# Moving a first pair of batches' outputs into the last two key-block pairs, and ordering products ahead of the moves out of their PSUM bank, in a one-core Perceiver block

## The chip, the core and the metric

The kernel runs on one core of one Trainium2 chip. A core has TensorE (PE: matrix products, with its weight loads shown apart as PEld), VectorE (DVE), ScalarE (ACT), GpSimd (POOL) and SyncE (SP, which here only issues transfers). Each engine works through its own instruction queue in order and waits on semaphores for the others. TensorE writes its results to PSUM, a memory of eight banks of 128 partitions by 512 float32 values; VectorE and ScalarE move them from there to SBUF, the main on-chip memory. DMA transfers between SBUF and HBM are issued from the queues of SP, ScalarE or GpSimd.

The metric is the device time of one execution in microseconds (us); lower is better.

## The reference, cut to what matters

All arithmetic is in float32. There are 4 batches of 256 tokens with 256 channels, and a context of 4096 rows with 192 channels for each batch. Three residual sublayers follow one another:

```python
x = x + cross_attention(layernorm(x), ctx)      # 16 heads of 16, 4096 keys
x = x + causal_self_attention(layernorm(x))     # 16 heads of 16, k and q normalised per head
x = x + slot_ffn(layernorm(x))                  # 64 slots, the 8 best for each token
```

The change is mostly in the third one:

```python
S = slot_init (64 slots, the same for each batch)
h = gelu(concat(x, mean(S)) @ w1 + b1)
logits = (h @ w2 + b2) / (abs(tau) + 0.1)
alpha = softmax over the 8 largest logits, 0 elsewhere        # tokens x slots
si = (alpha.T @ x) / alpha.sum(over tokens)                   # slots x channels
r, z = sigmoid(gates of si @ Wih.T + bih and S @ Whh.T + bhh)
n = tanh(i_n + r * h_n);  S_new = (1 - z) * n + z * S
y = layernorm(S_new + softmax(q(S_new) k(S_new).T / 8) v(S_new)) * ln_g + ln_b
out = alpha @ (y @ wvp + bvp) @ wo + bo
```

## The kernel before, in words

The order of the instructions on TensorE, VectorE and ScalarE is written out by hand: each queue holds its instructions in the order in which the Python code issues them, and a framework adds the waits. For PSUM it keeps engines apart by bank: a product into one half of a bank waits for a move out of the other half if the move was issued first.

Most of the time goes to the cross attention. Its 4096 keys come in chunks of 512, and the work is done in *blocks* of 128 keys and *pairs* of blocks: 16 pairs per batch, 64 in all. In a block (`cross_block`) TensorE computes scores into four pairs of banks (line 165), ScalarE takes their exponentials (line 1758 for the first pair of banks, in two halves; line 1760 for the three others), and TensorE weighs the values with them (line 179). The weighing of one pair is issued between the scores of the two blocks of the next pair. VectorE adds the weighed sums up (line 1774). The keys and values of the following chunk are computed meanwhile, in every pair but the last two, where no chunk follows.

The rest of the block is hung into these pairs by a dictionary, `plan`, with keys (batch of the loop, pair, place). While the loop goes through the keys of batch b, it does the remaining steps of batch b−1. From batch 1 on a loop has 17 pairs: pair 6 is the self attention of the previous batch (lines 1792, 1802 and 1823). Places 0 and 2 stand before the keys' or values' products of a pair, place 1 after them, place 4 at its end. A step gets the PSUM banks it may use; `x_` and `y` are the pairs of banks that the first and second exponentials of the pair's second block release. A step may be a generator; its later parts are issued at fixed points further on (`later`).

The steps that matter here, with their lines:

- Set-up, in the loop of batch 0: `set_logits` (line 1179) folds tau into `w2` and `b2` and the mean slot into `b1c`. `set_slots` (line 1203, three times) computes the gates' share that comes from the slots: two products into the two halves of one bank, and a move into `gh` after each (line 1212).
- Per batch: `self_out` makes `x2`, the input of the third sublayer; `hidden`, `routing` (line 1418 is its product) and `slot_inputs` (line 1460) follow, and `alpha_turned` (line 1486) makes `alphaT`, alpha transposed. Two batches share the partitions: an even batch has rows 0 to 63, an odd one rows 64 to 127.
- Per two batches: `gates` (three products with `wih`, each of half a bank, for r, z and n), `slot_qkv` with `slot_qk` and `slot_v` (q, k and v of the new slots), `slot_scores`, `slot_mix`, then `slot_values` (its result is `sv`, line 1630), and `give` for each batch: two products of `alphaT` with `sv` (line 1635), one addition of `x2` (line 1648), one transfer out (line 1640).

For batches 0 and 1, `gates` to `slot_mix` stand in the loop of batch 2 (pairs 13 to 16), `slot_values` in that of batch 3 at pair 5, and the two gives at its pairs 6 and 9. Batch 2's routing stands at pair 15 of batch 3, its `slot_inputs` and `alpha_turned` at pair 16.

After the last pair, `ending` (line 1864) does everything that is left: batch 3's last weighing (`cross_weigh`, into the two banks of `y`) and all its further steps, and the slots and outputs of batches 2 and 3 together. Each of its steps needs the one before. It ends with four products (lines 1635 and 2084), which give batch 3's and batch 2's outputs, two additions on VectorE (line 2095), two copies on ScalarE (line 2098) and four transfers, two from SP's queue and two from ScalarE's.

Where the listings number lines, these are the lines of the profile.

Of the kernel before, what the change touches and what calls it, by code (L numbers as in the profile page):

```python
# [900 lines left out]
def fast_(es, tc, nc, a, out, k, const, x0):  # L901
# [277 lines left out]
    def set_logits(bank):  # L1179
        rt = small.tile([P, 1], F32, name="rtau", tag="rtau")  # L1180
# [6 lines left out]

        m = small.tile([P, 2], F32, name="smean", tag="smean")
        nc.vector.tensor_reduce(m, slotsT[:, :, 0:SLOTS], AX.X, ALU.add)
        nc.vector.tensor_scalar(m, m, 1.0 / SLOTS, None, ALU.mult)  # L1190
        product(bank[:, 0:1], lambda c: w1[:, 2 + c, :], lambda c: m[:, c : c + 1])
# [11 lines left out]
    def set_slots(i, bank):  # L1203
        w = hold["whh"]
        for m in range(2):
# [4 lines left out]
            )  # L1210
            g = slice(2 * i + m, 2 * i + m + 1)
# [178 lines left out]
    def self_out(s, bank):  # L1390
# [6 lines left out]
        s.x2 = held.tile([P, QT, C], F32, name="x2", tag="x2")  # L1397
# [17 lines left out]
    def routing(s, bank):  # L1415

        for t in range(QT):
# [8 lines left out]
            small.tile([P, QT, n], F32, name=name, tag=name)  # L1426
# [66 lines left out]
    def gates(w, *room):  # L1493
# [5 lines left out]
        second = room[2] if len(room) > 2 else bank  # L1499
# [13 lines left out]
        pz = gate(2, second, int(second is bank))  # L1513
# [5 lines left out]
        pn = gate(4, other)  # L1519
# [15 lines left out]
    def slot_qk(w, bank, other):  # L1535
        w.fq, w.fk = (small.tile([DQ, S2], F32, name=n, tag=n, bufs=1) for n in ("fq", "fk"))
        q, k_ = bank[0:DQ, 0:S2], other[0:DQ, S2 : 2 * S2]
        for to, weights in ((q, fwq), (k_, fwk)):
            product(to, lambda c: weights[:, c, :], lambda c: w.snT[:, c, :])
        nc.scalar.activation(w.fq, q, AF.Identity, bias=fbq, scale=DQ**-0.5)  # L1540
        nc.vector.tensor_scalar(w.fk, k_, fbk, None, ALU.add)
# [7 lines left out]
    def slot_qkv(w, bank):  # L1549
        slot_qk(w, bank, bank)  # L1550
        slot_v(w, bank, 1)()
# [144 lines left out]
    for b in range(B - 1):  # L1696
# [5 lines left out]

        at = 4 if b == B - 2 else 0
# [17 lines left out]
            ((11 + at, 0), step(routing, s)),  # L1721
            ((12 + at, 0), step(slot_inputs, s)),
            ((12 + at, 1), step(alpha_turned, s)),
        ]
        if b % 2:
# [7 lines left out]
                ((NJ // 2 + 1 + 5, 0), step(slot_values, s.two)),  # L1733
                ((NJ // 2 + 1 + 6, 1), step(give, batches[b - 1])),
                ((NJ // 2 + 1 + 9, 1), step(give, s)),
            ]
        for (p, place), f in steps:
            plan[b + 1 + p // (NJ // 2 + 1), p % (NJ // 2 + 1), place] = f

# [124 lines left out]
    def ending(blocks, *pairs):  # L1864
# [134 lines left out]
        for t, bank in enumerate((x_0, x_1)):  # L1999
# [17 lines left out]
            held.tile([P, QT, C], F32, name=n, tag=n, bufs=b_) for n, b_ in (("x2", 2), ("x2n", 1))  # L2017
# [42 lines left out]
        slot_qk(both_, y_1, w_0)  # L2060
# [21 lines left out]
        for t, bank in enumerate((x_0, x_1)):  # L2082
            given(s, t, bank[:, 0:C])
            nc.tensor.matmul(
                w_1[:, t * C : (t + 1) * C],
                both_.alphaT[rows_of(d), t * P : (t + 1) * P],
                both_.sv[rows_of(d)],
                start=False,
                stop=True,
                skip_group_check=True,  # L2090
            )
        for t, bank in enumerate((x_0, x_1)):
            res, res_d = (temp()[:, 0:C].rearrange("p (t c) -> p t c", t=1) for _ in range(2))
            at = slice(t, t + 1)
            nc.vector.tensor_tensor(
                res, bank[:, 0:C].rearrange("p (t c) -> p t c", t=1), s.x2[:, at, :], ALU.add
            )
            nc.scalar.copy(res_d, halves(w_1)[:, at, :])
            send(s, at, res, nc.sync)
            send(d, at, res_d, nc.scalar)  # L2100
# [30 lines left out]
    for b, s in enumerate(batches):  # L2131
# [3 lines left out]
        for p in range(NJ // 2 + (b > 0)):  # L2135
# [22 lines left out]
            take(2, x_[:, 0, :], y[:, 1, :])  # L2158
            if not own and n + 1 < n_chunks:
# [74 lines left out]
```

## Time and profile before

| | |
|---|---|
| median of 3 runs | 860.78 us (857.23 to 861.16) |
| the profiled execution | 855.56 us |
| its span in the profile | 853.8 us |
| TensorE busy, share of the span | 826.6 us, 97% |
| ScalarE busy | 606.0 us, 71% |
| VectorE busy | 309.4 us, 36% |
| mean granted TensorE clock | 0.997 |
| written to HBM | 1.05 MB |

A line of a timeline gives the start in us from the span's start, the time until the last of its instructions ended, the engine, the line of the kernel and the operation, the tile written and the tiles read, the shapes, and how many instructions were merged into it (x16). A float32 product is recorded as two. In brackets stands how long the engine idled before it and what ended that wait. SPq and ACTq are the queues' own rows, here the issuing of transfers. All intermediate PSUM results are in one tile named `banks`.

### The profile page before, as it was taken

Reading aid. Unit: us, or ns where it says so; the run is one execution under the profiler, and the core shown is the slowest. Engines: PE = TensorE matmul, PEld = TensorE weight load, DVE = VectorE, ACT = ScalarE, POOL = GpSimd, SP = SyncE. Lnnn points to the kernel's source line nnn. Section 1 sums busy time; section 2 is a strip of 40 time slices with the busy share of each in tenths; the row PEclk is TensorE's granted clock in tenths of the full one; section 3 lists DMA queues with packets and bytes.
Section 4 is the critical chain, followed back from the end, with each engine's and each line's share of the span. In section 5 each row is a group of like instructions: output and inputs, shape, how many; then the busy total and the mean of one; then the engine's idle time right before and its main releaser. Section 6 shows DMA issues by size and latency. Waiting matters only on the chain.

```text
span 853.8 us, 18512 instructions
## 1 busy us (share of the span) xinstructions
PE 826.6 (97%) x7975; PEld 439.0 (51%) x7975; DVE 309.4 (36%) x760; ACT 606.0 (71%) x844; POOL 16.8 (2%) x20
## 2 busy tenths in 40 slices
PE   8999999999999999999999999989999999999885
PEld 5445545455555555545545555545555555444563
DVE  3133233232263352212254453232334433212664
ACT  5776766767677768777777777757777677877551
POOL 1000100000000010000000010000000000000000
PEclk9999999999999999999999999999999999999998
DMA  7600001000000000000000000000000101000000
GB/s 203 161 27 26 25 19 57 26 26 25 26 26 26 2 26 26 26 25 26 26 25 26 2 26 26 26 14 14 26 26 25 37 3 39 25 2 2 1 1 29
DMA packets 21850, 25.80 MB, mean 30 GB/s; under 512 B 6272, under 2 KB 13312, under 8 KB 21760
## 3 DMA queue, kind: packets, MB, share of 16 engines
q1 hardware_dynamic: 20800, 23.75, 9.6%
q8 instruction: 64, 1.05, 0.5%
q10 hardware_dynamic: 864, 0.79, 0.3%
q14 instruction: 26, 0.21, 0.1%
q0 software_dynamic: 96, 0.01, 0.0%
HBM read 23.48 MB, written 1.05 MB: 29 GB/s over the span
## 4 chain that ended last, share of the span: by engine, by line
PE 93%; ACT 3%; DVE 3%; issue 1%; ACTq 0%; DVEq 0%
PE banks L165 30%; PE banks L179 27%; PE banks L993 7%; PE banks L80 7%; PE banks L107 6%; PE banks L86 4%; PE banks L120 4%; PE banks L1823 1%; PE banks L981 1%; ACT prob L1760 1%; PE banks L194 1%; PE banks L1792 1%; PE banks L1460 1%; PE banks L1058 1%; ACT prob L1802 0%
## 5 line engine op out<-in xcount | busy, mean ns | idle before, releaser
L1760 ACT ACTIVATE prob<-banks 128x1024 f32<-128x1024 f32 x384 | 366.8, 1045 | 0.0
L165 PE MATMUL banks<-qh,kt 32*128 32x512 f32 x2048 | 267.3, 620 | 2.7 <-ACT prob L1760 1.5
L179 PE MATMUL banks<-prob,v 128*32 128x256 f32 x4096 | 234.3, 381 | 0.8 <-ACT prob L1802 0.5
L1758 ACT ACTIVATE prob<-banks 128x512 f32<-128x512 f32 x256 | 138.9, 595 | 131.4 <-PE banks L165 131.2
L179 PEld LDWEIGHTS banks<-prob,v 128*32 128x32 f32 x4096 | 126.6, 110 | 124.6 <-ACT prob L1758 45.8
L165 PEld LDWEIGHTS banks<-qh,kt 32*128 32x128 f32 x2048 | 103.9, 183 | 120.0 <-issue 69.2
L1774 DVE TENSOR_TENSOR sums<-banks,sums 128x512 f32<-128x512 f32 x120 | 82.6, 690 | 195.5 <-PE banks L179 166.4
L80 PE MATMUL banks<-ctx,wk 128*128 128x512 f32 x128 | 61.5, 603 | 0.1
L107 PE MATMUL banks<-wv,ctx 128*128 128x256 f32 x256 | 61.5, 383 | 0.0
L107 PEld LDWEIGHTS banks<-wv,ctx 128*128 128x128 f32 x256 | 46.9, 190 | 13.9 <-ACT prob L1758 6.8
L150 DVE COPY v<-banks 128x512 f32<-128x512 f32 x35 | 23.9, 690 | 79.9 <-PE banks L120 79.9
L94 DVE TENSOR_SCALAR kt<-banks,bk 128x512 f32<-128x512 f32 x32 | 24.0, 750 | 65.6 <-PE banks L86 65.6
L150 ACT COPY v<-banks 128x512 f32<-128x512 f32 x29 | 17.0, 586 | 32.7 <-PE banks L120 31.4
L86 PE MATMUL banks<-ctx,wk 64*128 64x512 f32 x128 | 37.0, 640 | 0.0
L95 ACT ACTIVATE kt<-banks,bk 128x512 f32<-128x512 f32 x32 | 22.1, 689 | 20.4 <-PE banks L86 19.6
L120 PE MATMUL banks<-wv,ctx 64*128 64x256 f32 x256 | 36.3, 402 | 0.0
L80 PEld LDWEIGHTS banks<-ctx,wk 128*128 128x128 f32 x128 | 20.9, 190 | 21.6 <-ACT prob L1760 11.9
L120 PEld LDWEIGHTS banks<-wv,ctx 64*128 64x128 f32 x256 | 22.0, 186 | 11.1 <-issue 9.6
L1807 DVE TENSOR_TENSOR prob<-prob,tri 128x512 f32<-128x512 f32 x32 | 20.8, 689 | 10.4 <-ACT prob L1802 9.8
L1802 ACT ACTIVATE prob<-banks 128x512 f32<-128x512 f32 (+1 forms) x30 | 17.9, 695 | 8.5 <-PE banks L1792 8.5
L987 DVE COPY tmp<-banks 128x512 f32<-128x512 f32 x17 | 11.8, 691 | 33.2 <-PE banks L981 33.2
L993 PE MATMUL banks<-wqkv,tmp 128*128 128x512 f32 (+1 forms) x64 | 23.0, 497 | 0.7 <-ACT prob L1802 0.5
(275 smaller groups left out, 505.6 us busy)
## 6 DMA issues: line engine op xcount, KB each, us to landing
ctx<-in_ctxT SPq DMA_DIRECT2D x32, 256.0 KB, 3.1
ctx<-in_ctxT SPq DMA_DIRECT2D x64, 128.0 KB, 3.2
x<-in_x SPq DMA_DIRECT2D x4, 256.0 KB, 3.4
wih<-in_ffn_WihT SPq DMA_DIRECT2D x1, 768.0 KB, 7.1
tmp<-in_ffn_WhhT SPq DMA_DIRECT2D x3, 256.0 KB, 5.7
out<-tmp SPq DMA_DIRECT2D x2, 256.0 KB, 2.2
wq<-in_L_xattn_Wq ACTq DMA_DIRECT2D x1, 256.0 KB, 5.9
wo<-in_L_xattn_Wo SPq DMA_DIRECT2D x1, 256.0 KB, 4.8
```

The lines of the kernel that those rows point to most:

```text
L80: nc.tensor.matmul(pk[c], k.wk[:, 0, c * P : (c + 1) * P], cx[:, 0, :], start=True, stop=False)
L86: nc.tensor.matmul(pk[c], k.wk[left(c), 1, c * P : (c + 1) * P], cx[left(c), 1, :], start=False, stop=True,)
L94: nc.vector.tensor_scalar(kt[:, 0, :], pk[0], k.bk[:, 0:1], None, ALU.add)
L107: nc.tensor.matmul(pv[n // 2][:, n % 2, :], cx[:, 0, n * P : (n + 1) * P], k.wv[:, 0, :], start=(n % 2 == 0), stop=False, skip_group_check ...
L120: nc.tensor.matmul(pv[u][:, i, :], cx[left(u), 1, n * P : (n + 1) * P], k.wv[left(u), 1, :], start=False, stop=True, skip_group_check=True,)
L150: copy(v[:, :, 0 : H * VW].rearrange("p i (h w) -> p i h w", w=VW)[:, :, :, 0:D], src.rearrange("p i (h d) -> p i h d", d=D),)
L165: nc.tensor.matmul(sc[:, m, :], kt[r, c, i * P : (i + 1) * P], qh[r, c, :], start=True, stop=True)
L179: nc.tensor.matmul(po[q * 32 : (q + 1) * 32, s * NQ : (s + 1) * NQ], v[:, i, w0 : w0 + 32], pr[s][:, m, e * NQ : (e + 1) * NQ], start=(fir ...
L993: nc.tensor.matmul(dst, lhs(c), rhs(c), start=(c == 0), stop=(c == 1))
L1758: nc.scalar.activation(pt[:, m, :], sc[:, m, :], AF.Exp)
L1760: nc.scalar.activation(pt, sc, AF.Exp)
L1774: nc.vector.tensor_tensor(s.sums[c], bank, s.sums[c], ALU.add)
```

## The change

It has these parts:

1. `set_logits`: the mean slot and its product are issued ahead of the six steps with tau.
2. `set_slots`: both products are issued before the two moves.
3. `gates`, where it has two banks: the second product goes to the other bank, and the third to the second half of the first bank.
4. `slot_qkv`: the products of q, k and v are issued first, then the three moves; for batches 0 and 1 the move of q (`fq`) goes from ScalarE to VectorE.
5. `slot_values` of batches 0 and 1 goes to pair 15 of batch 3's loop, ahead of batch 2's routing; their two gives go to pair 16, behind batch 2's `alpha_turned`. A new place 5 gives them four banks, after the second block's scores; the two gives use the banks that the last weighing uses next. Batch 2's routing, `slot_inputs` and `alpha_turned` move from places 0 and 1 to place 5 of the same pairs.
6. `x2` has three buffers in place of two; the four large tiles of `routing` have one in place of two.
7. `ending`: the four last products alternate between batches 2 and 3, with one bank for each batch; one addition, one copy and two transfers of 256 KB follow, batch 2's from SP's queue and batch 3's from ScalarE's.

```diff
     def set_logits(bank):
+        m = small.tile([P, 2], F32, name="smean", tag="smean")
+        nc.vector.tensor_reduce(m, slotsT[:, :, 0:SLOTS], AX.X, ALU.add)
+        nc.vector.tensor_scalar(m, m, 1.0 / SLOTS, None, ALU.mult)
+        product(bank[:, 0:1], lambda c: w1[:, 2 + c, :], lambda c: m[:, c : c + 1])
         rt = small.tile([P, 1], F32, name="rtau", tag="rtau")
...
-        m = small.tile([P, 2], F32, name="smean", tag="smean")
-        nc.vector.tensor_reduce(m, slotsT[:, :, 0:SLOTS], AX.X, ALU.add)
-        nc.vector.tensor_scalar(m, m, 1.0 / SLOTS, None, ALU.mult)
-        product(bank[:, 0:1], lambda c: w1[:, 2 + c, :], lambda c: m[:, c : c + 1])
         nc.vector.tensor_tensor(b1c, bank[:, 0:1], b1, ALU.add)
...
                 lambda c: slotsT[:, c, :],
             )
+        for m in range(2):
             g = slice(2 * i + m, 2 * i + m + 1)
             nc.vector.tensor_scalar(
                 gh[:, i, m, :],
...
-        s.x2 = held.tile([P, QT, C], F32, name="x2", tag="x2")
+        s.x2 = held.tile([P, QT, C], F32, name="x2", tag="x2", bufs=3)
...
-            small.tile([P, QT, n], F32, name=name, tag=name)
+            small.tile([P, QT, n], F32, name=name, tag=name, bufs=1)
             for name, n in (("lg", SLOTS), ("rest", SLOTS), ("best", 8), ("ex", SLOTS))
...
         bank, other = room[0], room[1]
-        second = room[2] if len(room) > 2 else bank
+        second = room[2] if len(room) > 2 else other
...
-        pz = gate(2, second, int(second is bank))
+        pz = gate(2, second)
...
-        pn = gate(4, other)
+        pn = gate(4, other if len(room) > 2 else bank, int(len(room) == 2))
...
-        nc.scalar.activation(w.fq, q, AF.Identity, bias=fbq, scale=DQ**-0.5)
-        nc.vector.tensor_scalar(w.fk, k_, fbk, None, ALU.add)
+
+        def move():
+            if w.last:
+                nc.scalar.activation(w.fq, q, AF.Identity, bias=fbq, scale=DQ**-0.5)
+            else:
+                nc.vector.tensor_scalar(w.fq, q, DQ**-0.5, fbq, ALU.mult, ALU.add)
+            nc.vector.tensor_scalar(w.fk, k_, fbk, None, ALU.add)
+
+        return move
...
     def slot_qkv(w, bank):
-        slot_qk(w, bank, bank)
-        slot_v(w, bank, 1)()
+        moves = slot_qk(w, bank, bank), slot_v(w, bank, 1)
+        for move in moves:
+            move()
...
-            ((11 + at, 0), step(routing, s)),
-            ((12 + at, 0), step(slot_inputs, s)),
-            ((12 + at, 1), step(alpha_turned, s)),
         ]
+        if b < B - 2:
+            steps += [
+                ((11, 0), step(routing, s)),
+                ((12, 0), step(slot_inputs, s)),
+                ((12, 1), step(alpha_turned, s)),
+            ]
...
-                ((NJ // 2 + 1 + 5, 0), step(slot_values, s.two)),
-                ((NJ // 2 + 1 + 6, 1), step(give, batches[b - 1])),
-                ((NJ // 2 + 1 + 9, 1), step(give, s)),
...
+    def first_more(x_0, x_1, y_0, y_1):
+        slot_values(batches[0].two, x_1)
+        return routing(batches[B - 2], x_0)
+
+    def second_more(x_0, x_1, y_0, y_1):
+        s = batches[B - 2]
+        slot_inputs(s, x_0)
+        alpha_turned(s, x_1)
+        for e, bank in zip(batches, (y_0, y_1)):
+            give(e, bank)
+
+    plan[B - 1, 15, 5], plan[B - 1, 16, 5] = first_more, second_more
...
-        for t, bank in enumerate((x_0, x_1)):
-            given(s, t, bank[:, 0:C])
-            nc.tensor.matmul(
-                w_1[:, t * C : (t + 1) * C],
...
-        for t, bank in enumerate((x_0, x_1)):
-            res, res_d = (temp()[:, 0:C].rearrange("p (t c) -> p t c", t=1) for _ in range(2))
-            at = slice(t, t + 1)
-            nc.vector.tensor_tensor(
-                res, bank[:, 0:C].rearrange("p (t c) -> p t c", t=1), s.x2[:, at, :], ALU.add
-            )
-            nc.scalar.copy(res_d, halves(w_1)[:, at, :])
-            send(s, at, res, nc.sync)
-            send(d, at, res_d, nc.scalar)
+        for t in range(QT):
+            for e, bank in ((d, w_1), (s, x_0)):
+                r = rows_of(e)
+                nc.tensor.matmul(
+                    bank[:, t * C : (t + 1) * C],
+                    both_.alphaT[r, t * P : (t + 1) * P],
+                    both_.sv[r],
+                    start=(e is s),
...
+        res, res_d = (halves(temp()) for _ in range(2))
+        nc.scalar.copy(res_d, halves(w_1))
+        nc.vector.tensor_tensor(res, halves(x_0), s.x2, ALU.add)
+        send(d, slice(0, QT), res_d, nc.sync)
+        send(s, slice(0, QT), res, nc.scalar)
...
             take(2, x_[:, 0, :], y[:, 1, :])
+            take(5, x_[:, 0, :], x_[:, 1, :], y[:, 0, :], y[:, 1, :])
```

## The prediction

> **What bounds the kernel now.** I read the page first, for the engine that fills the span and the chain that ended last; then the waits of each tile that the edit touches; then the timelines around those waits; then the last 80 us engine by engine.
>
> ```profile
> PE 826.6 (97%) x7975; PEld 439.0 (51%) x7975; DVE 309.4 (36%) x760; ACT 606.0 (71%) x844; POOL 16.8 (2%) x20
> ...
> PE 93%; ACT 3%; DVE 3%; issue 1%; ACTq 0%; DVEq 0%
> ```
>
> TensorE works through one fixed queue, and 93% of the chain is that queue. ScalarE, at 71%, waits for it in every pair of key blocks. So until the last two pairs, time taken out of TensorE's queue comes off the end. In the last two pairs and in the ending, dependencies decide. The timeline near 565 us shows the largest stall:
>
> ```profile
> 564.30 2.08 PE L165 MATMUL banks<-qh,kt 32*128 32x512 f32 x16
> 566.43 2.86 ACT L1760 ACTIVATE prob<-banks 128x1024 f32<-128x1024 f32 x3
> 566.79 0.60 PE L993 MATMUL banks<-snT,fwk 128*64 128x128 f32 x4
> 569.14 0.37 ACT L1540 ACTIVATE fq<-banks,fbq 64x128 f32<-64x128 f32 x1
> 569.54 0.34 DVE L1541 TENSOR_SCALAR fk<-banks,fbk 64x128 f32<-64x128 f32 x1 [3.55 <-ACT fq L1540]
> 569.94 1.13 PE L993 MATMUL banks<-fwv,snT 128*128 128x256 f32 x4 [2.54 <-DVE fk L1541]
> ```
>
> ScalarE's move of fq stands behind three exps; fk shares its bank and waits for it; TensorE's next product is in that bank too and waits for both. Smaller stalls of the same kind, a product waiting for the move out of its own bank, stand at the slot products and at the gates:
>
> ```profile
> 120.19 0.71 PE L993 MATMUL banks<-slotsT,tmp 128*128 128x128 f32 x4
> 121.47 0.71 PE L993 MATMUL banks<-slotsT,tmp 128*128 128x128 f32 x4 [0.56 <-DVE gh L1212]
> ...
> 552.24 1.16 PE L993 MATMUL banks<-siT,wih 128*128 128x128 f32 x8
> 553.98 2.05 PE L993 MATMUL banks<-siT,wih 128*128 128x128 f32 x16 [0.59 <-DVE gate_r L1511]
> ```
>
> The last two pairs have no keys and values to compute:
>
> ```profile
> 777.62 0.66 PE L1418 MATMUL banks<-w,hT 128*128 128x64 f32 x4
> 779.76 2.90 PE L165 MATMUL banks<-qh,kt 32*128 32x512 f32 x16 [1.48 <-ACT prob L1760]
> ...
> 788.31 2.86 ACT L1760 ACTIVATE prob<-banks 128x1024 f32<-128x1024 f32 x3
> 789.73 0.65 PE L1486 MATMUL banks<-ident,alpha 128*64 128x128 f32 x4
> 790.31 3.66 PE L179 MATMUL banks<-prob,v 128*32 128x256 f32 x64
> 790.75 0.29 DVE L1472 TENSOR_TENSOR siT<-banks,sden 128x128 f32<-128x128 f32 x1
> ```
>
> At 778 TensorE idles 1.48 us for an exp to release a bank; at 790 it goes from batch 2's transposed alpha into the last weighing with no gap.
>
> **The change, part by part.** I count by when TensorE's next instruction starts, since a recorded length holds a drain that overlaps its successor.
>
> *Slot set-up (three times).* A product that nothing delays hands over 0.54 us after its start (1.08 for the eight rows at 552.24). The second products now start then: 121.47 − 120.73 = 0.74, and by the same rows at 132.47 and 145.18 0.75 and 0.68. Sum −2.17. VectorE's first move starts 0.3 us later and the second earlier; what follows uses other banks.
>
> *Mean ahead of tau.* The product starts at 109.23; TensorE was done with the scores of 106.75 at about 108.75. The six tau and scale steps (107.56 to 108.64) go behind. Reduce (0.28) and scale (0.17) then end near 108.2: −0.48. w2, b2 and b1c are first used a batch later.
>
> *Gates.* The second gate goes to the other bank, which the third exp of the block releases at about 553.4. TensorE is ready at 553.30, so 0.15 us remain of 0.68: −0.53. The third gate takes the first bank's second half; gate_r's addition (553.50 to 553.92) is over before the second gate's product (about 554.5).
>
> *q, k and v before their moves.* TensorE could go on at 567.27 (k's product hands over after 0.48, as q's does from 566.31 to 566.79) and goes on at 569.94: −2.67. fq leaves ScalarE for VectorE, where it costs what fk does (0.34). The moves now wait for the product of v (568.3): fq, fk and fv end near 569.5. Behind them waits the scores product, which TensorE reaches at 572.73 − 2.67 = 570.06, so the cover is 1 us for fk; each microsecond beyond comes back. VectorE was idle there for 3.55 us.
>
> *Outputs moved out of batch 3's pairs 5, 6 and 9.* slot_values goes (666.46 to 667.42: −0.96), the first give (679.44 to 680.50: −1.06), and the second, which ran among key products: those take 1.92 us there (713.54 to 715.46) against 1.06 two pairs earlier (689.98 to 691.04), −0.86. Sum −2.88. ScalarE idles 0.9 to 2.4 us before the next groups of exps there, so it does not take the gain. Two additions leave VectorE and two sends SP's queue; the context loads there wait for TensorE anyway.
>
> *slot_values before the routing, pair 15.* 0.96 us. It waits for the second half of the first exp (777.9) and ends near 778.9, the routing near 779.6; the scores behind it wait for the exp until 779.76. I take 0; with the cover gone it is +0.96. VectorE's sv (0.48) and logits end near 780, and ScalarE takes the routing's exp only at 784.60.
>
> *The gives, pair 16.* TensorE now runs four products at 790.31 (their bank is free at 789.4), and the last weighing, in those same banks, waits for VectorE's addition of each. The first give takes 1.13 (row at 679.44), to 791.44; VectorE is through with siT at 791.04; the addition takes 0.69 (L1648's median, 688 ns), to 792.17. The weighing starts at 792.2 instead of 790.31: +1.9. The second addition ends near 792.9 and is needed at 794.0. Below: at the ending VectorE's addition starts 0.79 us after the first such product (844.33 to 845.12); 0.79 + 0.69 = +1.5. Above: the gives start only with the last exp's end at 791.17: +2.8. Everything behind is the ending, so this is all on the path. ScalarE's alphaT copy now waits for the gives (one buffer, old rows read first): from 791.02 to about 792.4; behind it stands a 1.28 us table load, and ScalarE's next work is at 795.95. SP's two sends wait for VectorE with nothing urgent behind them.
>
> *Buffers.* A third x2 holds batch 0's rows longer. The routing tiles go to one buffer; their uses are a batch apart, or 38 us before the last (788.1 against 826.6). 0.
>
> *The last transfers.*
>
> ```profile
> 845.58 1.92 SPq L1640 DMA_DIRECT2D out<-tmp  x2
> 846.43 0.37 ACT L2098 COPY tmp<-banks 128x256 f32<-128x256 f32 x1 [0.46 <-ACT tmp L2098]
> 846.83 0.66 ACTq L1640 DMA_DIRECT2D out<-tmp  x1
> ```
>
> Before, the last of four issues is at 846.83 and lands in 2.6 us. After, one copy (0.59 as for other 512-wide copies) and one addition (0.69) start at 845.5, so both issues come by 846.25. A 256 KB store landed in 2.2 us alone; with two at once I allow 3.1, as for the 128 KB ones on SP: 848.5 to 849.4 against 849.4. I take −0.2; bounds −0.9 and +0.5. The Trainium skill, "DMA: Bandwidth & Descriptors", section "Issuing engines are not separate DMA queues", says that queues share the same 16 DMA engines, so a second issuing engine saves only issue time. By that rule the same bytes leaving 0.5 us later end 0.5 us later, and the sum below would be −6.3; the rows of 846 to 849 us (143, 125, 273 GB/s) leave it open.
>
> **Sum:** −2.17 − 0.48 − 0.53 − 2.67 − 2.88 + 0 + 1.9 − 0.2 = −7.0 us. The profiled execution took 855.56 (span 853.8), so its like would take 848.6. It lies 5.2 below the median of the runs, 860.78, so against that median I say 853.8.
>
> **Rivals.**
> *The last pairs cost more:* +2.8 and +0.96 in place of +1.9 and 0. For it: both waits hang on ScalarE's release of banks. Against: the releases are 0.9 us early at both places. Gain 5.1, 855.7.
> *Part comes back:* stalls are counted in full only if the banks behind them are free; if a third of the 8.7 us taken out returns as waits for exps, and the last pairs cost 2.8, the gain is 5.8 − 2.8 + 0.2 = 3.2: 857.6, within 0.5% (4.3 us, about what a measurement tells from no change).
> *The exps pace the pairs:* then nothing taken out of TensorE's queue before pair 15 counts, and the added +1.9 remains: 862.5, slower than before; with the upper costs 2.8, 0.96 and 0.5, 865.0. It decides where ScalarE idles less per pair than TensorE loses. Against it: ScalarE idles 1.7 to 2.1 us before most second blocks, and after 569.5 for 3.86 us, more than each stall.
> *The transfers end later* (+0.5): 854.5.
>
> **Chances.** The forecast with its bounds, the dearer last pairs and the later transfers give gains over 4.3: 0.78. Part comes back: 0.16. Paced by exps: 0.06, of which I put all on slower to be safe. The range: with all bounds good the gain is 8.7 − 1.5 + 0.9 = 8.1, which from the lowest run, 857.23, gives 849.1; the profiled execution's like, 848.6, lies a little lower, so the low end is 848.5. With a third of the 8.7 back, dear last pairs and late transfers it is 5.8 − 2.8 − 0.5 = 2.5, from the median 858.3; the high end is 858.5.
>
> **What would show it.** After: no wait of TensorE on gh or fk; the gate wait near 0.15; no slot_values before pair 15 of batch 3; the gap at 778 filled; the last weighing released by VectorE's tmp about 0.8 us after the last give; two stores at the end. The prediction is wrong if the score products after the removed stalls wait longer for ScalarE than now, or if the last weighing starts over 3 us after the alpha product.

## The result, and the profile after

The kernel after takes 849.32 us (median of 4 runs, 848.42 to 850.32), where the kernel before took 859.28 beside it (4 runs, 857.23 to 861.16). The ratio is 0.9889, with a 95% interval from 0.9858 to 0.9919: 10.0 us faster. The prediction was 853.8 us and a gain of 7.0: right in sign and inside its range, but 4.5 us too high in time. The profiled execution of after took 850.10 us, with a span of 848.2; that of before had 853.8. So the two profiles differ by 5.6 us only, and the timed runs by 10. Both gaps, 5.6 against the predicted 7.0 and 10.0 against 7.0, have to be explained.

The page of after, its busy times and its chain of work:

```profile
PE 828.2 (98%) x7975; PEld 440.2 (52%) x7975; DVE 309.1 (36%) x760; ACT 605.7 (71%) x842; POOL 16.7 (2%) x20
...
PE 94%; ACT 2%; DVE 2%; issue 0%; ACTq 0%; DVEq 0%
```

TensorE bounds the kernel as before; its share of the chain rose from 93% to 94%, at the cost of the waits for ScalarE and VectorE (3% each before). It is even 1.6 us longer busy than before, although nothing was added to its work; the reason is below.

The timeline of after around the slots, the gates and q, k and v (start, time until the last ended, engine, line, operation; in brackets the idle time before and what ended it):

```profile
120.81 1.16 PE L993 MATMUL banks<-slotsT,tmp 128*128 128x128 f32 x8
...
550.39 3.26 PE L993 MATMUL banks<-siT,wih 128*128 128x128 f32 x24
...
563.93 0.65 PE L993 MATMUL banks<-snT,fwq 128*64 128x128 f32 x4
...
564.42 0.60 PE L993 MATMUL banks<-snT,fwk 128*64 128x128 f32 x4
564.95 1.13 PE L993 MATMUL banks<-fwv,snT 128*128 128x256 f32 x4
565.91 1.89 PE L107 MATMUL banks<-wv,ctx 128*128 128x256 f32 x8
566.19 0.34 DVE L1546 TENSOR_SCALAR fq<-banks,fbq 64x128 f32<-64x128 f32 x1 [2.58 <-PE banks L993]
566.46 0.33 DVE L1547 TENSOR_SCALAR fk<-banks,fbk 64x128 f32<-64x128 f32 x1
566.72 0.40 DVE L1555 TENSOR_TENSOR fv<-banks,fbv 128x256 f32<-128x256 f32 x1
567.73 0.33 PE L1567 MATMUL banks<-fk,fq 64*64 64x64 f32 x4
```

The eight slot products and the 24 gate products are each one unbroken group; no product waits for gh, gate_r or fk. TensorE goes from q to k to v and on to the values without a pause. VectorE's three moves run beside it, and the score product at 567.73 waits for none of them.

The timeline of after in the last two pairs:

```profile
770.64 1.13 PE L993 MATMUL banks<-w,yT 128*128 128x256 f32 x4 [0.24 <-ACT prob L1780]
771.61 0.55 PE L1419 MATMUL banks<-w,hT 128*128 128x64 f32 x4
772.48 2.90 PE L165 MATMUL banks<-qh,kt 32*128 32x512 f32 x16 [0.31 <-ACT prob L1782]
...
782.44 0.65 PE L1487 MATMUL banks<-ident,alpha 128*64 128x128 f32 x4
783.02 1.14 PE L1644 MATMUL banks<-sv,alphaT 64*128 64x256 f32 x8
784.24 0.36 ACT L1492 COPY alphaT<-banks 64x256 f32<-64x256 f32 x1 [0.35 <-PE banks L1644]
784.25 1.29 DVE L1657 TENSOR_TENSOR tmp<-banks,x 128x512 f32<-128x512 f32 x2 [0.50 <-PE banks L1644]
785.00 3.66 PE L179 MATMUL banks<-prob,v 128*32 128x256 f32 x64 [0.84 <-DVE tmp L1657]
```

The gap of 1.48 us ahead of the scores of pair 15 is now 0.24 + 0.31, with slot_values in it. The four products of the gives start at 783.02, and the last weighing waits 0.84 us for VectorE's first addition: it starts 1.98 us after the gives began, where before it had no gap.

The last products before, and the timeline of the end after:

```profile
844.33 0.48 PE L1635 MATMUL banks<-sv,alphaT 64*128 64x256 f32 x1
```

```profile
840.09 1.13 PE L2107 MATMUL banks<-sv,alphaT 64*128 64x256 f32 x8
841.31 0.58 ACT L2116 COPY tmp<-banks 128x512 f32<-128x512 f32 x1 [2.12 <-PE banks L2107]
841.37 0.69 DVE L2117 TENSOR_TENSOR tmp<-banks,x 128x512 f32<-128x512 f32 x1 [1.38 <-PE banks L2107]
841.92 0.37 SPq L1649 DMA_DIRECT2D out<-tmp  x1
842.09 0.40 ACTq L1649 DMA_DIRECT2D out<-tmp  x1
```

The two issues stand 1.83 and 2.00 us behind the start of the last products; before, the last of four stood 2.50 us behind it (844.33 to 846.83).

This profile also has something that the first profile of before lacks. Busy time by stretch in the ending of after (columns: stretch, its length, busy time of PE, PEld, DVE, ACT and POOL with counts, granted clock of TensorE, DMA share, GB/s):

```profile
823.00:824.00 1.00, 0.03 (x1) 0.03 (x1) 0.81 (x4) 0.00 (x0) 0.00 (x0) 1.00 0.00 0
824.00:826.30 2.30, 2.30 (x18) 2.06 (x19) 1.07 (x3) 0.16 (x1) 0.00 (x0) 1.00 0.00 0
826.30:829.70 3.40, 3.40 (x18) 3.40 (x18) 1.31 (x4) 0.62 (x2) 0.00 (x0) 0.51 0.00 0
```

For 3.4 us TensorE runs at half its clock, in the gates' 24 products, which take 4.57 us instead of 2.94. (That is also why it is longer busy.) The first profile of before has no such stretch ahead of its last product.

**A measure for all profiles.** To compare profiles I use four times of each: S, the start of the first transposes (L981; it moves by up to 1.5 us between executions), W, the start of the last weighing, F, the start of the last products, and the end of the span. W − S holds all pairs, F − W the ending, the tail what follows. "Half clock" says where TensorE ran at half clock for one such stretch, ahead of F.

| kernel | S | W − S | F − W | tail | half clock |
|---|---|---|---|---|---|
| before (first profile) | 6.75 | 783.56 | 54.02 | 9.47 | none |
| before_again | 6.73 | 783.55 | 54.03 | 9.69 | none |
| before_third | 7.03 | 784.95 | 54.01 | 9.81 | pair 15 |
| before_fourth | 7.33 | 785.09 | 54.04 | 9.94 | pair 15 |
| setup_only | 7.09 | 781.53 | 54.03 | 9.85 | pair 15 |
| qkv_only | 6.62 | 781.21 | 54.04 | 9.83 | none |
| moves_only | 7.09 | 783.16 | 55.35 | 9.80 | ending |
| end_only | 6.87 | 784.86 | 54.04 | 8.53 | pair 15 |
| before_gap_filled | 7.57 | 783.58 | 55.40 | 9.65 | ending |
| after (first profile) | 7.83 | 777.17 | 55.09 | 8.11 | ending |
| after_again | 8.00 | 777.20 | 55.31 | 8.09 | ending |
| after_warm | 6.98 | 777.19 | 53.96 | 8.17 | none |
| gives_late | 6.77 | 775.22 | 56.13 | 7.98 | ending |
| gives_late_pe | 6.55 | 775.38 | 53.96 | 8.01 | none |

The pairs lost 783.56 − 777.17 = 6.39 us, and the tail 9.73 (mean of the four profiles of before) − 8.1 = 1.6. That makes 8.0. Against it, the first profile of after started 1.08 us later (S) and lost 1.07 in the ending to the half clock: 8.0 − 2.2 = 5.8, and the 5.6 between the spans, with the tail of before's first profile at 9.47, is explained.

### The profile page after: what moved, and what is told of

Read it like the earlier page. It is cut to its first block, busy times and chain, and to the rows that moved or that the text cites. A ratio compares the mean times of both kernels' runs of the same rounds, so it can differ in the third digit from the quotient of the medians.

```text
span 848.2 us, 18509 instructions
## 1 busy us (share of the span) xinstructions
PE 828.2 (98%) x7975; PEld 440.2 (52%) x7975; DVE 309.1 (36%) x760; ACT 605.7 (71%) x842; POOL 16.7 (2%) x20
## 4 chain that ended last, share of the span: by engine, by line
PE 94%; ACT 2%; DVE 2%; issue 0%; ACTq 0%; DVEq 0%
PE banks L165 30%; PE banks L179 27%; PE banks L993 7%; PE banks L80 7%; PE banks L107 7%; PE banks L86 4%; PE banks L120 4%; PE banks L1845 1%; PE banks L981 1%; PE banks L194 1%; PE banks L1058 1%; ACT prob L1782 1%; PE banks L1814 1%; PE banks L1461 1%; ACT prob L1824 0%
```

## The experiments

The theories were these. *Rows*: the gain is the sum of the parts as the timelines show them. *Clock*: a part of what the timed runs differ by is stretches at half clock, which come and go behind gaps of TensorE. *Part comes back* and *the last pairs cost more* are rivals of the prediction.

**setup_only**: parts 1 to 3 of the change on the kernel before.

```diff
+        product(bank[:, 0:1], lambda c: w1[:, 2 + c, :], lambda c: m[:, c : c + 1])
         rt = small.tile([P, 1], F32, name="rtau", tag="rtau")
...
+        for m in range(2):
             g = slice(2 * i + m, 2 * i + m + 1)
...
-        second = room[2] if len(room) > 2 else bank
+        second = room[2] if len(room) > 2 else other
```

> Parts 1 to 3 alone (mean slot ahead of tau, slots' products ahead of their moves, gates' banks in turn). The theory 'rows' (time leaves TensorE's queue as the timelines of the two kernels show it: mean 0.46, slots 2.45, gates 0.54): 3.45 us faster than before, 0.996 of it; the prediction's own terms give 3.18. The theory 'part comes back' (a third returns as waits for exps): 2.3 us. The theory 'clock' (some of what the whole change gained is stretches at half clock that come or go with the phase of the work): the runs of one kernel fall into groups with granted clocks 0.001 to 0.003 apart, 1 to 2 us each, and the median can lie 1 to 2 us off the rows' figure to either side.

Median 854.9 us against 858.6, ratio 0.9955 (0.9933 to 0.9978). Its profile has a stretch at half clock in pair 15, as before_third and before_fourth have; against these two W − S falls from 785.02 to 781.53, that is 3.49. Rows said 3.45, the prediction's terms 3.18: nothing came back.

**qkv_only**: part 4 alone.

```diff
-        slot_qk(w, bank, bank)
-        slot_v(w, bank, 1)()
+        moves = slot_qk(w, bank, bank), slot_v(w, bank, 1)
+        for move in moves:
+            move()
```

> Part 4 alone (products of q, k, v ahead of their moves, fq on VectorE). 'Rows': 2.62 us faster (the prediction said 2.67), 0.997. 'Part comes back': 1.8 us. 'Clock', if the stall of 2.54 us at 567 us is what lowers the clock in the timed runs of before: up to 2 us more, 4.5 us, and a granted clock in this kernel's runs above that in the runs of before. The timeline at 565 us should show no wait of TensorE between the products of q, k and v.

Median 853.61 us, ratio 0.9937 (0.9917 to 0.9958): 5.0 us faster, twice what the rows give. In the profile the pairs around the edit move from +0.11 to −2.50 us against before, which is 2.61, as rows said; W − S fell by 2.35. The rest of the median goes with the clock: none of its six runs lay under 0.996, and against the three runs of before beside it that reached 0.997 (mean 855.6) its mean, 853.6, is 2.1 lower. With six runs I can't say that this edit keeps the clock up; it may be chance.

**moves_only**: parts 5 and 6 alone.

```diff
-                ((NJ // 2 + 1 + 5, 0), step(slot_values, s.two)),
-                ((NJ // 2 + 1 + 6, 1), step(give, batches[b - 1])),
-                ((NJ // 2 + 1 + 9, 1), step(give, s)),
...
+    plan[B - 1, 15, 5], plan[B - 1, 16, 5] = first_more, second_more
```

> Parts 5 and 6 alone (outputs of the first two batches in pairs 15 and 16, three buffers for x2). 'Rows', from the two kernels' timelines: pairs 5, 6 and 9 give 0.90 + 0.68 + 0.86 = 2.44, pair 16 takes 1.97: 0.5 us faster. The prediction's terms: 2.88 - 1.9 = 1.0 faster. 'The last pairs cost more': 0.9 slower. 'Clock': any of these plus or minus 1 to 2 us.

Median 857.69 us, ratio 0.9984 (0.9964 to 1.0005): the runs alone show no change. W − S falls by 0.40: rows, within 0.1. By itself this part is worth next to nothing in work: it takes 2.4 us out of the pairs and puts 1.98 us on the path to the last weighing. But all twelve runs lay between 856.47 and 859.43 us, at clocks of 0.994 to 0.996, while 10 of 24 runs of before beside it lay between 860.8 and 863.9, at 0.988 to 0.991. Busy time by stretch in the ending of moves_only:

```profile
835.30:836.80 1.50, 0.23 (x2) 0.00 (x0) 1.33 (x4) 0.10 (x1) 0.00 (x0) 1.00 0.00 0
836.80:838.50 1.70, 1.09 (x8) 0.86 (x9) 0.39 (x2) 0.36 (x1) 0.00 (x0) 1.00 0.00 0
838.50:841.90 3.40, 3.38 (x13) 2.68 (x13) 1.75 (x7) 1.69 (x3) 0.00 (x0) 0.50 0.00 0
```

The pause of 1.37 us that TensorE makes ahead of q's product (836.90) and one of 0.53 us ahead of the slots' scores (838.52) stand right before the half clock.

**end_only**: part 7 alone.

```diff
-            send(s, at, res, nc.sync)
-            send(d, at, res_d, nc.scalar)
+        res, res_d = (halves(temp()) for _ in range(2))
...
+        send(d, slice(0, QT), res_d, nc.sync)
+        send(s, slice(0, QT), res, nc.scalar)
```

> Part 7 alone (two transfers of 256 KB at the end, one copy, one addition). The prediction: 0.2 us faster (between 0.9 faster and 0.5 slower; by the rule that the bytes leave 0.5 us later, 0.5 slower). 'Rows', from the two profiles (last product to end of span 9.5 us before, 8.1 after): 1.36 us faster, 0.998. If neither, the profile's last issue and the stretch behind it show which of the two moved.

Median 856.7 us, ratio 0.9978 (0.9954 to 1.0001): by the runs alone the gain is not clear of noise. The tail is 8.53 us, against 9.47 to 9.94 in four profiles of before: 1.2 less, near the rows' 1.36 and far from the prediction's 0.2. The last issue starts 0.50 us earlier. Busy time by stretch behind the products, before:

```profile
846.50:847.00 0.50, 0.00 (x0) 0.00 (x0) 0.00 (x0) 0.30 (x1) 0.00 (x0) 1.00 0.75 256
847.00:847.50 0.50, 0.00 (x0) 0.00 (x0) 0.00 (x0) 0.00 (x0) 0.00 (x0) 1.00 0.68 227
847.50:848.00 0.50, 0.00 (x0) 0.00 (x0) 0.00 (x0) 0.00 (x0) 0.00 (x0) 1.00 0.08 23
848.00:848.50 0.50, 0.00 (x0) 0.00 (x0) 0.00 (x0) 0.00 (x0) 0.00 (x0) 0.55 0.94 334
848.50:849.00 0.50, 0.00 (x0) 0.00 (x0) 0.00 (x0) 0.00 (x0) 0.00 (x0) 0.50 0.64 211
```

and end_only:

```profile
848.50:849.00 0.50, 0.00 (x0) 0.00 (x0) 0.00 (x0) 0.00 (x0) 0.00 (x0) 1.00 0.89 311
849.00:849.50 0.50, 0.00 (x0) 0.00 (x0) 0.00 (x0) 0.00 (x0) 0.00 (x0) 1.00 0.98 336
849.50:850.00 0.50, 0.00 (x0) 0.00 (x0) 0.00 (x0) 0.00 (x0) 0.00 (x0) 1.00 1.00 342
850.00:850.50 0.50, 0.00 (x0) 0.00 (x0) 0.00 (x0) 0.00 (x0) 0.00 (x0) 1.00 0.43 133
```

The bytes go in one run of some 320 GB/s instead of two with a pause between (23 GB/s); yet counted from F their bulk ends at about the same time, some 4.6 us behind 844.33 and 845.77. The last transfer even lands later: 5.4 us behind F in end_only and 5.4 to 5.6 in the kernels after, against 5.1 to 5.4 in the kernels with four transfers. So the data is not what became shorter. SyncE's own records show what did. With four transfers its second issue is through 2.9 to 3.2 us behind F; with two its only one is through at 2.2. SyncE's first semaphore instruction after its issues comes 7.2 to 7.7 us behind F with four transfers and 5.7 to 6.3 with two, and in all fourteen profiles the span ends 2.26 or 2.27 us behind that. So the end follows SyncE's queue, and not the landing of the bytes: some 0.9 us of the gain is that SyncE is through with its issues earlier. What it does in the 3.5 to 4.7 us that follow, a little less with two transfers, is not shown.

The sum of the four parts, by W − S and the tail, is 3.49 + 2.35 + 0.40 + 1.2 = 7.4 (7.7 with the 2.61 of qkv_only's own place), and the whole change gives 6.39 + 1.6 = 8.0. By medians it is 3.7 + 5.0 + 0.9 + 1.9 = 11.5 against 10.0. The work adds up to within 0.6; the medians don't, since the clock is in them.

**before_again, before_third and before_fourth**: the kernel before, unchanged, for three further profiles; and **after_again**, the kernel after.

> The kernel before, unchanged, for a second profile. In 24 runs beside the first four experiments its time went from 854.5 to 863.9 us with granted clocks from 0.997 down to 0.988. Theory 'clock': the time follows the clock, and where this execution lies near 861 us with a clock near 0.990, its profile shows three or more stretches of about 3.5 us at half clock that the first profile lacks, each right behind a gap of TensorE; where it lies near 857 us at 0.996, one such stretch or none. Theory 'start or transfers': the span differs with no such stretch, and the difference stands before the first 10 us or behind the last product.

> The kernel after, unchanged, in enough runs to see its groups. 'Clock': two groups, near 850.2 us at 0.995 and near 848.5 us at 0.998, and none near 0.990, since its queue has neither the gap of 1.5 us in pair 15 nor the stall of 2.5 us at q, k and v. 'Rows' alone: one group, 7.8 us below the runs of before at their highest clock (some 857), that is 849.

> The kernel before, unchanged, once more for its profile. In 35 runs beside the experiments 12 lay between 860.8 and 863.9 us at clocks of 0.988 to 0.991, 15 near 857.5 at 0.996, 4 near 855.9 at 0.997. 'Clock': if this execution falls in the low group (1 chance in 3), its profile shows where three or more stretches at half clock stand: behind the gap at 778 us by one reading, behind the stall at 567 us by another, or in the ending. If it falls in the high group, it shows none or one of them, and the place of that one.

> The kernel before, unchanged, one last profile. The three profiles of it so far have no stretch at half clock ahead of the last product (855.56 and 855.81 us) or one, at 780.3 to 783.8 us, behind the gap of pair 15 (857.65 us); with that gap filled none of 12 runs lay in the low group. 'The gap of pair 15 begins the low group': if this execution lies near 862 us, it has the stretch at 780 us and two or more behind it, in the last weighing and the ending. 'Elsewhere': the stretches stand ahead of 776 us. If it lies near 857 us, nothing new follows for the low group.

The three of before took 855.81, 857.65 and 858.19 us. The first has no half clock ahead of its last product, the others one stretch each, and W − S says what it costs: 784.95 and 785.09 against 783.56, 1.4 to 1.5 us. Its place, in before_third:

```profile
777.92 0.66 PE L1418 MATMUL banks<-w,hT 128*128 128x64 f32 x4
780.06 4.28 PE L165 MATMUL banks<-qh,kt 32*128 32x512 f32 x16 [1.48 <-ACT prob L1760]
```

and its busy time by stretch:

```profile
778.60:780.10 1.50, 0.04 (x2) 0.04 (x2) 1.19 (x8) 1.50 (x3) 0.00 (x0) 1.00 0.00 0
780.30:783.70 3.40, 3.40 (x15) 1.57 (x14) 0.00 (x0) 2.31 (x4) 0.00 (x0) 0.51 0.00 0
```

It stands right behind the gap of 1.48 us at 778. The first profile of before has the same gap and no half clock behind it, so the gap alone is not enough. All nine such stretches, in nine profiles, last 3.41 us. The Trainium skill, "TensorE: Matmul & The Clock Gate", Part 1, says that the clock is set by a free-running window of 4096 cycles, 3413 ns: the length agrees. So do the starts: in each of the nine profiles the half clock that sets in behind the last product begins a whole number of 3.413 us behind the start of the stretch (17.06 us or 5 in after, 71.68 us or 21 in before_third), while the place in the kernel differs. Where that grid lies when the gap comes could be why the same gap counts in one execution and not in another, but idle time in a window alone does not decide: the gap of 1.48 us lies whole in one window both in before and before_again, without half clock behind it, and in before_third, before_fourth, setup_only and end_only, with it. With 1.9 us idle in one window (moves_only, before_gap_filled, after_again, gives_late) the half clock followed all four times. The section "HAM oscillation" of the same page of the Trainium skill gives as the rule to leave no gap over about 3.4 us; here gaps of 1.48 us, and in after's ending 0.98 us, were enough, so for this kernel that limit is too high; what else in a window counts is not shown.

The six runs of after_again fell into two groups, three at 847.8 to 848.2 us (clock 0.997) and three at 850.1 to 850.4 (0.995), none near 0.990; its profile is of the lower clock and has one stretch, in the ending. Ratio 0.9888 (0.9863 to 0.9913), as the first time.

None of the four profiles of before caught a run near 862 us. Where its further stretches stand (from 855.5 to 862 would be four or five of these) stays open.

**after_warm**: idle products in four gaps of after's ending.

```diff
-        fill(z_0, 0.43)
+        fill(z_0, 1.29)
...
-        fill(z_0, 1.29)
+        fill(z_0, 1.72)
...
-        fill(x_1, 1.72)
+        fill(x_1, 2.58)
...
-        fill(x_0, 1.29)
+        fill(x_0, 2.15)
```

> The kernel after with idle products added in four gaps of its ending (at 800, 817, 823 and 832 us: 0.86, 0.43, 0.86 and 0.86 us more of products whose result nobody reads). 'Clock': the gaps no longer lower the clock, all runs lie in the group of 0.998, near 848.5 us; against the after runs in the lower group 1.7 us faster. 'Rows': TensorE's queue gets 3 us of work in gaps where it waited 1.08, 0.77, 0.98 and 0.87 us: no change where the gap holds it, or 0.1 to 0.3 us slower.

Median 848.12 us (847.88 to 848.64, six runs), ratio 0.9880 (0.9857 to 0.9903): one group, at the upper one of after_again; no half clock ahead of F in its profile, and F − W back at 53.96. Three microseconds of added work cost nothing and took the second group away. With the six runs of gives_late_pe below, where gaps of the ending are filled too, 12 of 12 runs lie in the upper group, against 5 of 10 of after. So for the ending the runs show the cause: gaps in TensorE's work, and hardly chance.

**before_gap_filled**: idle products in the gap of pair 15 of the kernel before.

```diff
+    def filled(s, bank):
+        fill(bank, 1.29)
+        return routing(s, bank)
...
-            ((11 + at, 0), step(routing, s)),
+            ((11 + at, 0), step(filled if at else routing, s)),
```

> The kernel before with 1.46 us of idle products in the gap of 1.48 us that TensorE has in pair 15 at 778 us (ahead of batch 2's routing); no work is removed. Reading 'the gap of pair 15 brings the low group': no run near 861 us at 0.990, all between 854.5 and 859 us at 0.994 or more, and a mean of all runs 1.5 to 2 us below that of before. Reading 'the stall at q, k and v brings it' or 'the ending brings it': one run in three still lies near 862 us. 'Rows' alone: no change, or up to 0.3 us slower.

Median 858.03 us (855.9 to 858.9), ratio 0.9994 (0.9973 to 1.0014). None of the twelve runs lay near 861 us, and W − S is 783.58, without a stretch. But ten of the twelve had a clock of 0.993 or 0.994, the profile shows a stretch in the ending instead, and the mean, 857.8 against 858.1 for before beside it, is not the 1.5 to 2 us lower that this reading promised. So the runs near 862 go with the gap of pair 15, and filling it alone wins nothing: in the profile the clock drops in the ending then. Over all experiments, the kernels in which something stands in that gap (after_again, after_warm, moves_only, before_gap_filled and the two below, and the first four runs of after) had 0 of 52 runs at a clock of 0.991 or less. Before had 16 of the 53 beside the experiments, and of the three others that keep the gap end_only had 3 of 12, setup_only 1 of 7 and qkv_only 0 of 6. How the gap leads there is not shown, as no such run was profiled.

**gives_late**: the kernel after, with the two gives moved from pair 16 into the ending.

```diff
-        for e, bank in zip(batches, (y_0, y_1)):
-            give(e, bank)
...
         next(route)
-        fill(x_1, 1.72)
+        first = list(zip(batches, (z_0, x_0)))
+        for e, bank in first:
+            for t in range(QT):
+                given(e, t, bank[:, t * C : (t + 1) * C])
+        fill(x_1, 1.29)
         finish(route)
+        for e, bank in first:
+            res = halves(temp())
+            nc.scalar.copy(res, halves(bank))
+            nc.gpsimd.tensor_tensor(res, res, e.x2, ALU.add)
+            send(e, slice(0, QT), res, nc.sync)
```

(alphaT gets two buffers; batch 3's x2 a temporary, and three small tiles one buffer each, to make room.)

> The kernel after, with the two gives of the first batches moved once more, from pair 16 (where they hold up the last weighing) into the ending, in place of idle products at 821 us; ScalarE copies their banks, GpSimd adds x2, and alphaT has two buffers. 'Rows': the last weighing starts 1.97 us earlier (1.14 of products and 0.84 of waiting for VectorE go), nothing is added elsewhere: 847.4 us where after has 849.3. 'Clock': plus or minus 1.7 us by the group. If the copies at 823 us or the smaller buffers delay something, less than 1.97.

Median 847.48 us, ratio 0.9869 (0.9845 to 0.9892). W − S fell by 1.95 to 1.98, as said: the gives did cost that in pair 16. In the ending, however, 0.8 us came back. Its timeline there:

```profile
820.10 0.29 DVE L1449 TENSOR_REDUCE asum<-lg 128x2 f32<-128x128 f32 x1
820.29 2.53 POOL L2082 TENSOR_TENSOR tmp<-tmp,x 128x512 f32<-128x512 f32 x2 [3.17 <-ACT tmp L2081]
820.62 1.08 DVE L1452 TENSOR_TENSOR alpha<-lg,asum 128x128 f32<-128x128 f32 x1
821.76 0.66 PE L1461 MATMUL banks<-alpha,sumto 128*128 128x64 f32 x4 [0.99 <-DVE alpha L1452]
```

The product that makes alpha, 0.29 us in after, takes 1.08 while GpSimd adds. GpSimd's first addition ends at 821.55, and the product 0.15 us behind it, at 821.70.

**gives_late_pe**: the same, with x2 added by TensorE, and two gaps filled as in after_warm.

```diff
-        fill(z_0, 1.29)
+        first = list(zip(batches, (z_0, z_1)))
+        for e, bank in first:
+            for t in range(QT):
+                nc.tensor.matmul(
+                    bank[:, t * C : (t + 1) * C], ident, e.x2[:, t, :], start=(t == 0), stop=False,
+                    skip_group_check=True,
+                )
...
-            nc.gpsimd.tensor_tensor(res, res, e.x2, ALU.add)
```

> As the run before with the gives in the ending, but TensorE adds x2 (as products of the identity, in place of the idle products at 816 us) instead of GpSimd, ScalarE's copy goes out directly, and two other gaps hold 0.86 us more of idle products. 'Rows': the addition that makes alpha took 1.08 us beside GpSimd's two additions there, 0.29 without them in after; if GpSimd was the cause, 0.29 again, and 0.8 us faster than that kernel; with the last weighing 1.98 us earlier than in after. 'Clock': the ending's gaps are filled, so all runs in the upper group: 846.0 us, where after's upper group has 848.0. If the alpha addition still takes 1 us, GpSimd was not the cause.

Median 846.0 us (845.72 to 847.01), ratio 0.9860 (0.9830 to 0.9891): 3 us faster than after (medians 849.3 and 849.1), and faster than both kernels of this case. In its timeline:

```profile
781.35 0.65 PE L1487 MATMUL banks<-ident,alpha 128*64 128x128 f32 x4
781.93 3.66 PE L179 MATMUL banks<-prob,v 128*32 128x256 f32 x64
...
820.56 0.29 DVE L1452 TENSOR_TENSOR alpha<-lg,asum 128x128 f32<-128x128 f32 x1
```

The last weighing follows the alpha product without a wait, and the product that makes alpha is back at 0.29 us without GpSimd beside it. F − W is 53.96 and no half clock stands ahead of F. Against after_warm W − S fell by 1.81, where 1.98 was expected. No run of after was taken beside these six, but all six lie below the lowest of after's ten (847.82).

## Why the prediction was right, and where it was wrong

**The stalls.** Slots: 0.82 + 0.84 + 0.79 = 2.45 gained at the three places against 2.17 worked out; the eight rows hand over after 1.00 us (120.81 to 121.81), where 1.08 was taken for them. Mean: 0.46 against 0.48. Gates: 0.54 against 0.53. q, k and v: 2.62 against 2.67. setup_only and qkv_only give the same alone, within 0.1 us.

**The outputs taken out of pairs 5, 6 and 9.** By the starts of the products behind each place the three gave 0.87 + 0.69 + 0.86 = 2.42 against 2.88. The term that failed is pair 6, 1.06. The scores behind the first give, before:

```profile
680.50 2.08 PE L165 MATMUL banks<-qh,kt 32*128 32x512 f32 x16
```

and after:

```profile
673.65 2.45 PE L165 MATMUL banks<-qh,kt 32*128 32x512 f32 x16
674.11 0.30 PEld L165 LDWEIGHTS banks<-qh,kt 32*128 32x128 f32 x4 [0.16 <-ACT prob L1824]
674.83 0.44 PEld L165 LDWEIGHTS banks<-qh,kt 32*128 32x128 f32 x8 [0.42 <-ACT vself L1348]
```

The first give gone, the scores start 1.06 us earlier, but the group takes 2.45 us instead of 2.08: its weight loads now wait for ScalarE, for the last exp of the self attention and for the move of `vself`, which the give had covered. The step that failed is that ScalarE "does not take the gain" because it idles before the next exps: in pair 6 that idle time was 1.09 us, and after it is gone. Pair 9 held, and pair 5 gave 0.09 less.

**The last two pairs.** slot_values in pair 15: 0, as worked out; the cover was the exp's release of its bank, and it held. The gives in pair 16: 1.97 against 1.9, with the wait for VectorE at 0.84 against the 0.8 named. The rival "the last pairs cost more" is out.

**Part comes back, the exps pace the pairs.** W − S fell by 6.39, where the terms up to the last weighing made 6.83, and of the 0.44 that is missing pair 6 has 0.37, pair 5 0.09, the gives 0.07, q, k and v 0.05, while the slots gave 0.28 more; 0.07 comes back at 606 us in after and 0.04 behind pair 9. So "part comes back" is seen, but in pair 6 with 0.37 us and not with a third of the 8.7. "The exps pace the pairs" is not seen.

**The last transfers.** The term −0.2 failed by its size: the tail fell by 1.2 alone and by 1.6 in after. The last issue came 0.50 us earlier, near the 0.58 that was worked out; the step that was wrong put the landing of the bytes at the end of the span. In before 4.8 us of the span lie behind the bulk of the bytes (849.0 to 853.8), and its end follows SyncE's queue, which is through with issuing 0.9 us earlier when it has one transfer instead of two. The rival "the transfers end later", and with it the estimate of −6.3 from the Trainium skill ("DMA: Bandwidth & Descriptors", section "Issuing engines are not separate DMA queues"), is out for the time. What that section states of the bytes is not contradicted: the last landing came 0.3 us later behind F (means 5.5 against 5.2), and with two large transfers at once the traffic stayed at some 320 GB/s, what before reached in its best stretch (334).

**The median.** The step that cost most is the last one: that the profiled execution lies 5.2 us below the median of before and that after would keep this distance. Its own figure for a like execution, 848.6, lies among the runs of after, 847.8 to 850.4. That this fits so well is in part luck: the profiles give 8.0 us of work where the sum had 7.0, and after loses time to a half clock (1.1 to 1.3 us in its two profiles) that the prediction did not have. The measured median lies only 0.8 us above the low end of the range. The 5.2 us were no constant. By the clocks of the 53 later runs they go with half clock: 45 lie at 0.996 or less, and the profiled execution at 0.997 had no stretch ahead of its last product. The three runs behind 860.78 have no clock on record, and no run near 861 was profiled, so for them this is argued and not shown. Counted in means, 53 runs of before beside the experiments took 858.7, and its eight runs at a clock of 0.997 855.5; after's ten runs took 849.2, and the five at its upper clock 848.2. So before loses about 3.2 us to them and after about 1.0: of the 9.5 us between the means, by this count, 7.3 are work and 2.2 the clock; S, which was 7.8 and 8.0 in the two profiles of after against 6.7 to 7.3 in those of before, may be why the 7.3 is less than the 8.0 of the profiles. That the work moved into the gap of pair 15 has its share in that is supported by the 0 of 52; how much each part of the change gives of the 2.2 was not measured.

## What to carry to other kernels

Time that is added by small gaps is not only their length: a gap of 1 to 1.5 us in TensorE's work could set it to half clock for the next 3.4 us, so look at the granted clock in fine stretches behind each gap, and fill the gap with waiting work or, where none is ready, with idle products. Before a predicted gain is subtracted from a median, find out by what the profiled execution and the other runs differ; if it is the clock, the change may keep, lose or gain it. An operation that has to go somewhere near the end belongs into a gap of the dependent tail, and not on the full queue ahead of it: the two gives cost 2 us in pair 16 and nothing in place of idle products. At the end of a program ask which queue is through last, and not only when the bytes land.

## What the runs showed of the hardware that was not expected

- The half clock behind short gaps: 3.41 us in each of nine profiles, at a price of 1.1 to 1.5 us each. In each of them the half clock behind the last product starts a whole number of 3.413 us later.
- VectorE beside GpSimd: the product of two operands in SBUF took 1.08 us instead of 0.29 while GpSimd added two operands of 128 x 512. The reduction just before, with one operand, started 0.19 us ahead of GpSimd and took its usual 0.29. Here, and for an operation with one operand in SBUF that met another addition of GpSimd in after (line 1667, 1.02 us, its like behind it 0.28), VectorE's operation ended 0.15 us behind GpSimd's addition, as if it had waited for the whole of it. The Trainium skill, "GPSIMD Engine Reference", section "Specifications", says that the two engines share their interfaces to SBUF and contend where VectorE has two inputs in SBUF or runs in a mode that takes two ports; for two inputs the run agrees.
- The end of the program: with two transfers instead of four and the same bytes, which landed no earlier, the tail was 1.2 to 1.6 us shorter. In all fourteen profiles the span ended 2.26 or 2.27 us behind the first semaphore instruction in SyncE's queue after its last issue.
